# A decoder layer on one core: the first feed-forward product made as features by tokens, with its layer norm applied behind the second product

## The chip, the core and the metric

The kernel runs on one core of a Trainium2 chip. A core has TensorE (PE: matrix products into PSUM; PEld is its loading of weights), VectorE (DVE), ScalarE (ACT), GpSimd (POOL, which reaches SBUF but not PSUM) and SyncE (SP, which here issues DMAs). Each engine works through its own instructions in their order and waits on semaphores for the others. The metric is the device time of one execution in microseconds; the median of the runs shown counts.

## What is computed

x is 128 sequences of 128 tokens by 256 features; ctx has the same shape. The layer is self-attention, cross-attention and a feed-forward part, each on a layer norm of x and each added to x; both attentions have 16 heads of 16 features. The part that matters here, cut from the reference:

```python
def layernorm(x, w, b, eps=LN_EPS):
    mu = jnp.mean(x, axis=-1, keepdims=True)
    var = jnp.mean((x - mu) ** 2, axis=-1, keepdims=True)
    return (x - mu) * jax.lax.rsqrt(var + eps) * w + b
h = jnp.einsum('btd,hd->bth', x, absmean(W_fc))      # 256 -> 1024
h = jax.nn.gelu(h, approximate=False)
h = layernorm(h, ln_w, ln_b)                         # over the 1024
return jnp.einsum('bth,dh->btd', h, absmean(W_proj)) # 1024 -> 256
```

absmean makes a matrix of −1, 0 and 1 from the weights. The layer norm stands between the two products, over the 1024 hidden features of each token.

## The kernel before

The 128 sequences are taken in 32 groups of G = 4 rows, a row being one sequence of 128 tokens. The kernel is written as streams (Python generators), each of which issues a few instructions and yields: A is the attention of all groups, one row at a time, first the maxima of the scores (`maxima`, L680), then transposed scores (L752), exponentials (`weights`, L778) and outputs (L797); n prepares a group for self-attention, k the keys and values of the context, c the queries of the cross-attention, and f (`finish`, L581) projects the cross-attention's result, adds it to x and does the feed-forward part; w and t prepare constants and weights; x, y and z (`finish_rows`, L608) do the feed-forward part of the last group in pieces of 2, 1 and 1 rows.

The order of all work is written out by hand as strings of these letters: `START + ORDER * (n_groups - 4) + END` (L860). So ORDER is repeated 28 times, and within each engine the instructions stand in the order of the letters. Nothing is reordered later. In one repetition 36 steps of A, 36 steps of f (before) and the steps of n, k and c alternate, so that the attention of one group runs beside the feed-forward part of an earlier one.

PSUM has eight banks. Two tiles of two banks hold scores, one bank holds the attention's outputs, and three banks (`bank`, L194) serve every other product in turn; a product can start only when the bank that it gets has been read.

The feed-forward part of a group, before, has two pairs of rows:

- `transposed` (L290) computes the layer norm of x (statistics on VectorE, rstd and `apply` on GpSimd, L281, L282 and L286) and transposes the result on TensorE (pt, L304). `split` (L429) makes two parts of it, a rounded one (fp32r) and its remainder, so that products in fp32r keep their precision.
- `hidden` (L434) makes the first product tokens by features: the 128 tokens of a row are the stationary operand, 512 columns of `w_fc` the moving one, four matmuls per bank (two parts by two chunks of 128 input features, L443). ScalarE applies gelu from PSUM into g (L450). VectorE takes the statistics of g over the 1024 features (L275, L276), GpSimd makes rstd, and g is normalised in place, row 0 by VectorE and row 1 by GpSimd (L286).
- `second` (L469) transposes g in blocks of 128 by 128 on TensorE into PSUM (pg, L477; 16 per pair). From there ScalarE writes the rounded part times ln_w (L486) and VectorE the remainder (L488, one input from PSUM, one from SBUF). Sixteen matmuls per row of these parts with `w_proj` (py, L501) make the result, and VectorE adds it to x (L510). ln_b times `w_proj` is the constant row `b_proj` (L537 to L547), added by GpSimd (`add_row`, L421).

Gelu and Exp need different tables on ScalarE. The kernel asks for Gelu's at L438 and Exp's at L452; where a function follows that isn't in the table that is loaded, the build puts in a further load.

All transfers but two at the start are issued by SP, in the order of the letters: per group the next x, the context, the rearrangement of the attention's outputs (sums, o_raw), the factors by way of DRAM (by_head, factors) and the output (L602).

Of the kernel before, what the change touches and what calls it, by code (L numbers as in the profile page):

```python
# [27 lines left out]
P = 128  # L28
D = 256
# [24 lines left out]
    "nnnnnnwnwnnnwnnnAnAAnnAwnAAnAnAnAAAAAnnAAknnwAnnnnwnccnkAnnAAnnAnAkAcccckcAAcAnAAkccAccccntAAkAAnkAn"  # L54
    "AnAAnAkckAnnAnAcAnAnAnntAnAAAckccAccckkAAknAkAnknAnckcnAcAActAAftkAAAncAcAAntAAAffffAffnAnfnAnnAAnAn"
    "kAffnAAkfcfAffkfAAfknncffAAffffAkkfAnfcAcnfAfAffAAccfAc"
)
ORDER = (
    "ncfAfffAAkkAccAAcfcAnnfAAAccAffAAnnkAAnnAnfAnkAAAfffAfffnAAkcnnAnnAnAfkfkcAffffffAAfffAfffAfccccfffA"
    "fkfkAAAncfAn"  # L60
)
END = (
    "cfAfAffAfAcAcffcAfAAckAAxcAkcfffAAfffAAkfAAAAAkffkAcfAcAfffffAffAffccfffAcckcfckfAffAfAkkAfcAcfAAffc"
    "cAcfcAfAfkAAffAkAkfkAAAAfAfAffffAAxxAffAxAfffAxfffyfAfffffyfxAyffffAfxyxxxzxyfxfffzffyxzzffxxxxyyzxx"
    "yyzzzyzzz"
# [4 lines left out]
def tile_decoder_layer(ctx: ExitStack, tc: tile.TileContext, a: dict, out: bass.AP):  # L70
# [55 lines left out]
    with nc.allow_non_contiguous_dma(reason="a few hundred bias elements, once"):  # L126
# [18 lines left out]
        for src, shape in ((a["w_fc_t"], [P, CC, FF]), (a["w_proj_t"], [P, FC, D])):  # L145
            raw = p_one.tile(shape, F32, name="raw_w", tag="g", bufs=2)
            nc.sync.dma_start(raw, src.rearrange("(c p) o -> p c o", p=P))
            raw_weights.append(raw)
# [66 lines left out]
    def output_bias(w):  # L215

        pb = bank("pb")
        bv_cols = p_one.tile([P, CC, P], F32, name="bv_cols", tag="g_0")
# [5 lines left out]
    def masks():  # L224
        ident_32 = p_one.tile([P, 32], F32, name="ident_32", tag="g_0")
# [208 lines left out]
    def hidden(xn_parts, j0, n_rows=2, at=0):  # L434

        terms = [(i, c) for c in range(CC) for i in range(2)]
        g = p_one.tile([P, 2, FF], F32, name="g", tag="g", bufs=2)
        nc.scalar.preload_act_table(AF.Gelu)  # L438
        for j in range(n_rows):
            for n in range(FF // 512):  # L440
                ph = bank("ph")
                for i, c in terms:
                    nc.tensor.matmul(  # L443
                        ph,
                        xn_parts[i][:, c, (j0 + j - at) * P : (j0 + j - at + 1) * P],
                        w_fc[:, c, n * 512 : (n + 1) * 512],
# [3 lines left out]
                nc.scalar.activation(g[:, j, n * 512 : (n + 1) * 512], ph, AF.Gelu)  # L450
                if j + n == n_rows:
                    nc.scalar.preload_act_table(AF.Exp)  # L452
                yield
        agg = p_stat.tile([P, 2, 2], F32, name="agg", tag="agg", bufs=6)
        if n_rows == 2:
# [13 lines left out]
    def second(x, g, j0, n_rows=2):  # L469
# [29 lines left out]
        for j in range(n_rows):  # L499
# [8 lines left out]
            if j < n_rows - 1:  # L508
                yield
# [396 lines left out]
```

## Time and profile before

| what | us |
|---|---|
| median of 3 runs (lowest, highest) | 2737.69 (2736.14, 2737.96) |
| span of the profiled execution, first to last instruction | 2733.8 |
| TensorE busy | 2676.2 (98%) |
| VectorE busy | 2118.7 (78%) |
| ScalarE busy | 1579.2 (58%) |
| GpSimd busy | 1337.1 (49%) |
| length of one repetition of ORDER | 82.8 |

The profiled execution has no time of its own beside its span; the median is 3.9 us above that span. A row of the groups of instructions reads: line, engine, operation, what it writes and reads, the count, then busy time, mean length of one in ns, and the idle time just before them with what ended it. In a timeline a row is the start in us, the length, engine, line and operation; xN joins N instructions that follow each other. Means of matmuls overlap, since one starts before the former has ended; the distance of their starts is what one costs.

### The profile page before, as it was taken

The numbers are of one execution on the slowest core, as the hardware profiler recorded it, in microseconds if no ns is written. First come the engines' busy times: TensorE is split into PE (matmuls) and PEld (weight loads), VectorE is DVE, ScalarE is ACT, GpSimd is POOL, SyncE is SP. The second block draws the span as 40 slices with busy tenths as digits, with TensorE's granted clock in tenths as the row PEclk, the third lists the DMA queues.
The fourth block names the chain that finished last, engine by engine and source line by source line (L and its number), as shares of the span: only waits on it lengthen the run. The fifth ranks groups of instructions, "written<-read, shape, count | busy, mean of one in ns | idle before, by whom it ended". The sixth has DMA issues, their size and how long they took to land.

```text
span 2733.8 us, 77048 instructions
## 1 busy us (share of the span) xinstructions
PE 2676.2 (98%) x32845; PEld 1917.3 (70%) x32845; DVE 2118.7 (78%) x3916; ACT 1579.2 (58%) x2508; POOL 1337.1 (49%) x1425
## 2 busy tenths in 40 slices
PE   7999999999999999999999999999999999999998
PEld 4567777677777767776777776777777777777666
DVE  5677787777787777887777887777877778877777
ACT  3455666655665655665556666556656556665446
POOL 3344554544554554554445545445545445545443
PEclk9999999999999999999999999999999999999999
DMA  4121111221111221122211112211112211212210
GB/s 118 33 50 42 41 41 50 57 57 34 46 44 50 57 58 28 46 49 51 58 42 41 42 50 57 58 42 42 42 49 58 58 31 44 49 49 50 50 26 16
DMA packets 110093, 130.28 MB, mean 48 GB/s; under 512 B 32312, under 2 KB 69048, under 8 KB 109752
## 3 DMA queue, kind: packets, MB, share of 16 engines
q1 hardware_dynamic: 109464, 125.11, 19.0%
q8 instruction: 259, 4.24, 0.6%
q14 instruction: 82, 0.67, 0.1%
q10 hardware_dynamic: 288, 0.26, 0.0%
HBM read 71.38 MB, written 18.84 MB: 33 GB/s over the span
## 4 chain that ended last, share of the span: by engine, by line
PE 89%; DVE 7%; issue 2%; POOL 1%; ACT 1%; DMA 0%; ACTq 0%; DVEq 0%; SPq 0%; POOLq 0%
PE st L761 10%; PE av L806 9%; PE pq L324 9%; PE s L700 9%; PE ph L443 9%; PE py L501 8%; PE pk L324 8%; PE po L336 8%; PE pv L336 8%; PE pt L304 3%; PE pg L477 2%; PE s L689 2%; PE st L785 2%; DVE mx L711 1%; DVE g L488 1%
## 5 line engine op out<-in xcount | busy, mean ns | idle before, releaser
L711 DVE TENSOR_REDUCE mx<-s 128x8 f32<-128x1024 f32 x512 | 601.3, 1216 | 83.0 <-PE s L700 82.5
L794 ACT ACTIVATE w_t<-st 128x1024 f32<-128x1024 f32 x512 | 496.7, 1022 | 202.5 <-PE st L785 122.3
L281 POOL TENSOR_SCALAR rstd<-agg 128x4 f32<-128x4 f32 (+2 forms) x163 | 39.0, 239 | 965.5 <-DVE agg L276 965.5
L286 POOL TENSOR_SCALAR xn<-x,agg,rstd 128x256 f32<-128x256 f32 x378 | 458.4, 1226 | 9.9
L771 DVE COPY_PREDICATED_SCALAR st<-masked_t,masked_score 128x1024 f32 x256 | 316.1, 1280 | 68.1 <-PE st L761 68.1
L414 POOL TENSOR_TENSOR o_raw<-o_raw,factors 128x256 f32<-128x256 f32 x252 | 181.0, 745 | 382.9 <-DMA factors<-by_head 277.0
L809 ACT COPY raw<-av 128x512 f32<-128x512 f32 x256 | 151.0, 590 | 315.3 <-PE av L806 310.4
L486 ACT ACTIVATE g<-pg,ln_w 128x256 fp32r<-128x256 f32 (+1 forms) x520 | 205.8, 473 | 175.8 <-PE pg L477 163.6
L700 PE MATMUL s<-kt,qt 32*128 32x256 f32 x4096 | 298.8, 402 | 3.2 <-ACT w_t L794 2.2
L501 PE MATMUL py<-w_proj,g 128*128 128x256 f32 x2048 | 279.6, 289 | 1.3 <-DVE g L488 0.8
L806 PE MATMUL av<-w_t,v 128*32 128x128 f32 x8192 | 276.9, 276 | 0.5 <-DVE q_max L733 0.5
L806 PEld LDWEIGHTS av<-w_t,v 128*32 128x32 f32 x8192 | 209.0, 109 | 96.7 <-issue 80.0
L443 PE MATMUL ph<-w_fc,xn 128*128 128x512 f32 x1024 | 259.8, 404 | 4.2 <-ACT g L450 1.6
L501 PEld LDWEIGHTS py<-w_proj,g 128*128 128x128 f32 x2048 | 254.1, 189 | 13.2 <-issue 1.3
L286 POOL TENSOR_SCALAR g<-g,agg,rstd 128x1024 f32<-128x1024 f32 x63 | 241.1, 3828 | 6.6
L488 DVE SCALAR_TENSOR_TENSOR g<-pg,ln_w,g 128x256 fp32r<-128x256 f32 (+1 forms) x520 | 212.6, 469 | 30.3 <-ACT g L486 29.9
L700 PEld LDWEIGHTS s<-kt,qt 32*128 32x128 f32 x4096 | 187.8, 185 | 63.7 <-issue 40.2
L443 PEld LDWEIGHTS ph<-w_fc,xn 128*128 128x128 f32 x1024 | 184.8, 188 | 58.7 <-DVE xn L432 10.0
L761 PEld LDWEIGHTS st<-q_max,kt 32*128 32x128 f32 x4096 | 129.2, 186 | 61.1 <-DVE negm_self L722 42.5
L275 DVE BATCH_NORM_STATS2 stats<-g 128x6 f32<-128x512 f32 x256 | 160.9, 670 | 0.8 <-ACT g L450 0.8
L450 ACT ACTIVATE g<-ph 128x512 f32<-128x512 f32 x256 | 146.5, 599 | 25.3 <-PE ph L443 24.2
L761 PEld LDWEIGHTS st<-qt,kt 32*128 32x128 f32 x4096 | 128.1, 186 | 46.3 <-DVE mx L711 26.4
(130 smaller groups left out, 4612.8 us busy)
## 6 DMA issues: line engine op xcount, KB each, us to landing
o_raw<-raw SPq DMA_DIRECT2D x504, 64.0 KB
factors<-by_head SPq DMA_DIRECT2D x126, 256.0 KB
ctx_t<-in_ctx_t_dram SPq DMA_DIRECT2D x32, 512.0 KB
x<-in_x_dram SPq DMA_DIRECT2D x31, 512.0 KB
out_dram<-x SPq DMA_DIRECT2D x31, 512.0 KB
sums<-raw SPq DMA_DIRECT2D x126, 16.0 KB
by_head<-r SPq DMA_DIRECT2D x63, 32.0 KB
raw_w<-in_w_fc_t_dram SPq DMA_DIRECT2D x1, 1024.0 KB
```

The source lines that it names most:

```text
L286: engine.tensor_scalar(dst[:, j], src[:, j], agg[:, j, 0:1], rstd[:, j : j + 1], ALU.subtract, ALU.mult)
L324: nc.tensor.matmul(out, w[:, c, o * P : (o + 1) * P], src_t[:, c], start=(c == 0), stop=(c == CC - 1))
L336: nc.tensor.matmul(rows[:, j], src_t[:, c, (j0 + j) * P : (j0 + j + 1) * P], w[:, c], start=(c == 0), stop=(c == CC - 1),)
L443: nc.tensor.matmul(ph, xn_parts[i][:, c, (j0 + j - at) * P : (j0 + j - at + 1) * P], w_fc[:, c, n * 512 : (n + 1) * 512], start=((i, c) == ...
L488: nc.vector.scalar_tensor_tensor(parts[1][:, f0 + f, tok], pieces[:, f], scales[f], parts[0][:, f0 + f, tok].bitcast(F32), ALU.mult, ALU.s ...
L501: nc.tensor.matmul(rows[:, j], parts[i][:, f, j * P : (j + 1) * P], w_proj[:, f], start=((i, f) == terms[0]), stop=((i, f) == terms[-1]),)
L700: nc.tensor.matmul(s[r // 2][:, r % 2, 2 * o : 2 * o + 2], qt[strip, o, tok], kt[strip, o, :, tok], start=(stage == "self"), stop=True, sk ...
L711: nc.vector.tensor_reduce(mx[:, 2 * half : 2 * half + 2], s[half], AX.X, ALU.max, negate=True)
L761: nc.tensor.matmul(s[r // 2][:, r % 2, n], kt[strip, n // 2, n % 2, tok], added[strip, n // 2, n % 2] if stage == "self" else qt[strip, n ...
L771: nc.vector.copy_predicated(s[half].rearrange("p r n q -> p (r n) q"), masked_t[:, None, :].to_broadcast([P, 8, P]), masked_score[:, :, No ...
L794: nc.scalar.activation(w_t[:, 2 * half : 2 * half + 2], s[half], AF.Exp)
L806: nc.tensor.matmul(av[32 * r : 32 * r + 32, n], v[:, j, head : head + 32], w_t[:, r, n], start=True, stop=True)
```

## The change

The first product is turned round. The weights `w_fc` are now the stationary operand, in blocks of 128 hidden features, and the 256 tokens of a pair of rows the moving one, so that the result in PSUM is features by tokens and g comes out as the second product needs it: there is no transpose of g. Since the layer norm is over the features, which now lie along the partitions, it moves behind the second product: with shift = −mean, the result is (h·ln_w·w_proj + shift·w_sum)·rstd + b_proj, where `w_sum` is the row ln_w times `w_proj`, made once.

```diff
-        g = p_one.tile([P, 2, FF], F32, name="g", tag="g", bufs=2)
         nc.scalar.preload_act_table(AF.Gelu)
-        for j in range(n_rows):
-            for n in range(FF // 512):
-                ph = bank("ph")
+        for f0 in range(0, FC, n_f):
+            ph = bank("ph")
+            for f in range(n_f):
                 for i, c in terms:
                     nc.tensor.matmul(
-                        ph,
-                        xn_parts[i][:, c, (j0 + j - at) * P : (j0 + j - at + 1) * P],
-                        w_fc[:, c, n * 512 : (n + 1) * 512],
+                        ph[:, f * width : (f + 1) * width],
+                        w_fc[:, c, (f0 + f) * P : (f0 + f + 1) * P],
+                        xn_parts[i][:, c, tok],
...
-                nc.scalar.activation(g[:, j, n * 512 : (n + 1) * 512], ph, AF.Gelu)
...
-            statistics(g, (0,), FF, agg)
...
-            apply(nc.gpsimd, g, g, agg, rstd, 1)
...
-        apply(nc.vector, g, g, agg, rstd, 0)
...
+            g = p_one.tile([P, 512], F32, name="g", tag="g", bufs=4)
+            nc.scalar.activation(g, ph, AF.Gelu)
+            for f in range(f0, f0 + n_f):
+                piece = g[:, (f - f0) * width : (f - f0 + 1) * width]
+                scale = ln_w[:, f : f + 1]
+                nc.scalar.activation(parts[0][:, f, 0:width], piece, AF.Copy, scale=scale)
                 nc.vector.scalar_tensor_tensor(
-                    parts[1][:, f0 + f, tok],
-                    pieces[:, f],
-                    scales[f],
-                    parts[0][:, f0 + f, tok].bitcast(F32),
+                    parts[1][:, f, 0:width],
+                    piece,
+                    scale,
+                    parts[0][:, f, 0:width].bitcast(F32),
                     ALU.mult,
                     ALU.subtract,
                 )
+            if f0 == 0:
+                nc.scalar.activation(totals[:, 1], g, AF.Square)
+                before = g
+            else:
+                squares = p_one.tile([P, 512], F32, name="sq", tag="sq", bufs=2)
+                nc.scalar.activation(squares, g, AF.Square)
+                nc.gpsimd.tensor_tensor(totals[:, 0], before, g, ALU.add)
+                nc.gpsimd.tensor_tensor(totals[:, 1], totals[:, 1], squares, ALU.add)
+                before = totals[:, 0]
+            if f0 + n_f == FC:
+                nc.scalar.preload_act_table(AF.Exp)
             yield
+        while n_f > 1:
+            n_f //= 2
+            half = n_f * width
+            for i in range(2):
+                nc.gpsimd.tensor_tensor(
+                    totals[:, i, 0:half], totals[:, i, 0:half], totals[:, i, half : 2 * half], ALU.add
+                )
+        return parts, totals
+
+    def moments(totals, n_rows=2):
+
+        sums = bank("sums")[:, 0 : 2 * n_rows * P].rearrange("p (i j t) -> p i j t", i=2, j=n_rows)
+        for i in range(2):
+            for j in range(n_rows):
+                nc.tensor.transpose(sums[:, i, j], totals[:, i, j * P : (j + 1) * P], ident)
+        total = p_stat.tile([P, 2, n_rows], F32, name="total", tag="total", bufs=1)
+        nc.vector.tensor_reduce(total, sums, AX.X, ALU.add)
+        shift = p_stat.tile([P, n_rows], F32, name="shift", tag="shift", bufs=2)
+        nc.vector.tensor_scalar(shift, total[:, 0], -1.0 / FF, None, ALU.mult)
+        square = p_stat.tile([P, n_rows], F32, name="square", tag="square", bufs=1)
+        nc.vector.tensor_tensor(square, shift, shift, ALU.mult)
+        nc.vector.scalar_tensor_tensor(square, total[:, 1], 1.0 / FF, square, ALU.mult, ALU.subtract)
+        rstd = p_stat.tile([P, n_rows], F32, name="rstd", tag="rstd", bufs=6)
+        nc.gpsimd.tensor_scalar(rstd, square, 0.0, LN_EPS, ALU.max, ALU.add)
+        nc.gpsimd.tensor_tensor(rstd, rstd, minus_half.to_broadcast([P, n_rows]), ALU.pow)
+        return shift, rstd
...
-                    nc.tensor.transpose(
-                        pieces[:, f, j * P : (j + 1) * P],
-                        g[:, j, (f0 + f) * P : (f0 + f + 1) * P],
-                        ident,
-                    )
...
-        nc.vector.tensor_tensor(x[:, j0 : j0 + n_rows], x[:, j0 : j0 + n_rows], rows, ALU.add)
+            yield
+        shift, rstd = moments(totals, n_rows)
+        yield
+        for j in range(n_rows):
+            nc.vector.scalar_tensor_tensor(
+                rows[:, j], w_sum, shift[:, j : j + 1], rows[:, j], ALU.mult, ALU.add
+            )
+            nc.vector.scalar_tensor_tensor(
+                x[:, j0 + j], rows[:, j], rstd[:, j : j + 1], x[:, j0 + j], ALU.mult, ALU.add
+            )
```

So after each gelu ScalarE writes the rounded part of two blocks and the square of g, VectorE writes the remainders, and GpSimd adds up g and its squares over the eight blocks. The matmuls of the second product (py) follow, then `moments` transposes the totals, VectorE sums them up, GpSimd makes rstd, and four operations of VectorE per pair bring the result into x. The bank of py is held until then.

`finish` now runs `hidden` and `second` of the first pair, then of the second; before, it ran `hidden` of both pairs and then `second` of both. The f stream has 26 steps per group instead of 36, and all three strings of letters are new:

```diff
 ORDER = (
-    "ncfAfffAAkkAccAAcfcAnnfAAAccAffAAnnkAAnnAnfAnkAAAfffAfffnAAkcnnAnnAnAfkfkcAffffffAAfffAfffAfccccfffA"
-    "fkfkAAAncfAn"
+    "nkAfAcAAfnfAAkcfAcnckAAcfcAAAcknAkAnnAfffAAnnAAnfAfAfnfcnAnnAAnfkAnAfknfAfcfAAffccAfAfnfAffkAAAffcccA"
+    "fk"
 )
...
-        gs = []
         for j0 in range(0, G, 2):
-            gs.append((yield from hidden(xn_parts, j0)))
-        for j0, g in zip(range(0, G, 2), gs):
-            yield from second(x, g, j0)
+            parts, totals = yield from hidden(xn_parts, j0)
+            yield from second(x, parts, totals, j0)
```

The preparation of the ternary weights works in pieces of 512 columns instead of whole matrices, with other buffers, and makes `w_sum` beside `b_proj` (16 more matmuls, once). In the last group's pieces of one row a bank of ph holds four blocks of 128 columns.

## The prediction

> **What bounds the kernel now.** I read the page's first two parts, then the groups by shape, then a stretch of the repeated order and the timelines of ScalarE, VectorE and GpSimd in it. TensorE is the limit: busy 98% of the span, at full clock in all 40 slices.
>
> ```profile
> span 2733.8 us, 77048 instructions
> PE 2676.2 (98%) x32845; PEld 1917.3 (70%) x32845; DVE 2118.7 (78%) x3916; ACT 1579.2 (58%) x2508; POOL 1337.1 (49%) x1425
> PEclk9999999999999999999999999999999999999999
> ```
>
> One repetition of ORDER (28 of them) is a window of 82.85 us, in which TensorE idles 0.36 us; the others have room on average (columns: length, then busy time of PE, PEld, DVE, ACT, POOL):
>
> ```profile
> 1356.60:1439.45 82.85, 82.49 (x1029) 59.28 (x1025) 65.18 (x120) 49.22 (x79) 41.58 (x44) 1.00 0.18 45
> ```
>
> So time taken from TensorE is gained in full, if nothing in the new order makes it wait. These groups are touched (count | busy us, mean ns | idle before); a mean overlaps its neighbour, so I price matmuls by the spacing of starts:
>
> ```profile
> L477 PE MATMUL pg<-ident,g 128*128 128x128 f32 x1024 | 142.1, 276 | 3.6 <-DVE g L286 2.0 <-DVE g L488 1.2 <-DVE xn L432 0.4
> L443 PE MATMUL ph<-w_fc,xn 128*128 128x512 f32 x1024 | 259.8, 404 | 4.2 <-ACT g L450 1.6 <-DVE v L372 1.2 <-DVE g L488 1.1
> L501 PE MATMUL py<-w_proj,g 128*128 128x256 f32 x2048 | 279.6, 289 | 1.3 <-DVE g L488 0.8 <-ACT g L450 0.5
> L286 POOL TENSOR_SCALAR g<-g,agg,rstd 128x1024 f32<-128x1024 f32 x63 | 241.1, 3828 | 6.6
> L414 POOL TENSOR_TENSOR o_raw<-o_raw,factors 128x256 f32<-128x256 f32 x252 | 181.0, 745 | 382.9 <-DMA factors<-by_head 277.0 <-issue 105.0
> L438 ACT ACT_TABLE_LOAD x65 | 83.4, 1283 | 1.1
> ```
>
> Two places show something that the averages hide. While weights are prepared, VectorE runs an operation with two inputs in SBUF beside a GpSimd add or product with two inputs in SBUF:
>
> ```profile
> 120.60 3.61 POOL L414 TENSOR_TENSOR o_raw<-o_raw,factors 128x256 f32<-128x256 f32 x2 [2.24 <-DMA factors<-by_head]
> 120.93 2.70 DVE L535 SCALAR_TENSOR_TENSOR w_fc<-raw_w,half,below 128x2048 fp32r<-128x2048 f32 x1
> 161.48 3.28 POOL L414 TENSOR_TENSOR o_raw<-o_raw,factors 128x256 f32<-128x256 f32 x3 [9.02 <-DMA factors<-by_head]
> 161.91 1.56 DVE L540 TENSOR_TENSOR b<-ln_b,b 128x1024 fp32r<-128x1024 f32 x1
> ```
>
> Alone, the second L535 (w_proj) took 2.35 us and a GpSimd product 0.73. Here L535 took 0.35 more, what was left of the first product; the second product then waited until L535 had ended at 123.63: 3.61 us for what otherwise takes 1.46. At 161.9 it happens again. So these two kinds of instruction exclude each other, and take turns. The kernel before hardly ever mixes them: its L488 reads one input from PSUM.
>
> **The change, part by part** (per repetition, thus per group of four rows).
>
> TensorE: 32 transposes pg go, at 0.118 us (4 from 1457.31 to 1457.75, 8 from 1453.42 to 1454.39): −3.8. The 32 ph matmuls of 512 columns at 0.2425 (16 from 1439.40 to 1443.28), 7.8 us, become 64 of 256 columns. Nearest row: py, also 256 columns, 0.121 to 0.136 per matmul; I take 0.125, 8.0 us (ends 7.7 to 8.7). Eight transposes of totals add 0.9. Net −2.6 (−2.9 to −1.9): 80.25 us if TensorE never waits.
>
> VectorE: statistics of g (8 × 0.64 + 4 × 0.2 us) and its apply (2 × 1.0) go, −7.9; the wide add into x (2 × 0.69) becomes eight 256-wide operations at 0.45 and, twice, one reduction (0.65, as the 512-wide L510) and three tiny operations at 0.16: +4.3. Net −3.6 of 65. The 16 operations that make parts[1] keep their 0.42 us, but now read both inputs from SBUF.
>
> ScalarE: eight squares at about 0.55 (spacing of the 512-wide gelus) add 4.4. The built program has 193 table loads instead of 131, two more per repetition, because an Exp of the attention now falls between the third and fourth gelu of the second pair: +2.6. The copies read SBUF instead of PSUM; no row shows that, so 0.365 (spacing of L486) to 0.47 (its length) each, and I take the former. 49.2 becomes about 56.
>
> GpSimd: the applies of g go, −7.6; 12 additions of 512 columns come at 1.22 to 1.46 (256 columns take 0.73, of which up to 0.24 may be fixed, as in L281), I take 1.25; plus four of 256: +18. 41.6 becomes about 52.
>
> On average all fit into 80. But these pieces lie in the first 38 us after a group's first ph, where TensorE's order has this without waits (us after that ph): four ph steps until 6.1, py j=0 8.1 to 10.2, py j=1 10.5 to 12.5, totals 13.5; second pair ph 15.1, 19.3 to 21.3 and 23.5, py 27.5 to 29.5, pn 31.6, py 31.8 to 33.9, pt 37.4. I followed what each waits for:
>
> 1. First pair, ScalarE: load done at 1.5; each step holds it 1.86 (gelu 0.6, two copies 0.365, square 0.5), raw 0.59 between: third gelu ends at 6.35, and po waits for its bank: 0.25 lost.
> 2. First pair, sharing: from the second gelu's end (3.95) GpSimd has 9.0 us of additions, and VectorE six parts[1] operations among them. If a pair of these goes between two additions, the last ends near 11.5 where py j=0 wants it by 10.1, and the additions end at 15.6: about 1.85 lost. In strict turns the last ends at 14.8: about 4.7.
> 3. Second pair: x is now updated by four operations (1.9 us) after a reduction, and behind them on VectorE stand two parts[1] operations and the masking (2 × 1.25) that releases the attention's st: 0.7 lost.
> 4. Then on ScalarE, from the third ph's end (20.8): gelu step 1.86, gelu step 1.96, load 1.28, two Exp 1.94, load 1.28, gelu 0.6 is 8.9, ready 29.7. py, whose bank that gelu empties, would come at 28.4: 1.3 lost. Behind it queue the Exps for the next av.
> 5. The maxima L711 (2.35) stand behind the last parts[1]: 0.7, with sharing 1.35.
> 6. Statistics of the next x come behind those; GpSimd's rstd (1.3) and four applies (4.85) make xn 0.85 late for pt.
>
> Without sharing 3.8 us; with pairs 6.3; with strict turns, followed through the second pair too, 10.2. The rows say that turns are taken, but not whether VectorE keeps the port for two in a row; its L488 operations start 0.39 apart (four in 1.65 us) though 0.47 long, so I put the sum near the lower of the two: 7.0. Repetition: 80.25 + 7.0 = 87.25, that is +4.4; 28 × 4.4 = +123. The rest of a repetition has slack: there every wait in the order is met before its time by this addition. On SP's queue the output DMA waits later with x (VectorE ready 44 us after the first ph); by_head and factors of the next projection queue behind it, and are first needed 10 us later: nothing.
>
> Outside ORDER: three groups in START and END gain 2.6 each if not held up, −8; w_sum costs 16 matmuls (2.4) and 2.7 us on VectorE once, +4; the last pieces lose a statistics and eight transposes for additions on GpSimd, ±5. Sum −4, with ±15.
>
> Sum: the profiled span 2733.8, and 3.9 around it to the median of the three runs, 2737.7. 2737.7 + 123 − 4 = 2857.
>
> One rule speaks against the change still more. The row first: 65 table loads took 1283 ns each with 1.1 us idle before all of them, and the gelu follows within 0.01 us. The Trainium skill, "ScalarE: Activation LUTs", section "What ACT_TABLE_LOAD costs", adds a drain of about 1380 ns to each switch. By it, the two further loads of item 4 would cost 2.8 us more in each repetition, 28 × 2.8 = 77, and the estimate would be 2934; the trace shows no drain, and the sum leaves it out.
>
> **The rivals.**
> - Strict turns: 80.25 + 10.2 is +7.6 per repetition, 2947. For it: the second product waited out all of L535. Against: no row has two VectorE operations queued.
> - No sharing of note, only ScalarE's chain (items 1, 3 to 6): 84.05, +1.2 × 28 − 4, 2767. For it: L771 with two constants in SBUF keeps 1.21 to 1.29 beside GpSimd work.
> - Faster: the waits are absorbed, because ScalarE's steps from SBUF overlap more than PSUM's rows show and py finds its pieces. It decides below 2.6 us lost per repetition, at item 4 first; with half of that lost 2697, with none 2661. For it: VectorE and GpSimd are lighter or idle on average; TensorE certainly gets less work.
> - The transposes don't go: no; 1024 become 256, that is in the program.
>
> **How the numbers follow.** Forecast 0.42 (own range 2800 to 2915, for 5 to 9 us lost per repetition), strict turns 0.16, chain alone 0.18, faster 0.20, within 0.2% (about what a measurement of this kernel can tell from no change) 0.04. Slower 0.76. The range from 2690 to 2955 leaves out about half of the faster case and the end of strict turns.
>
> **What would show it.** Right: pg gone and TensorE's busy time near 2600, but a repetition of 87 us; waits of py for parts[1] and gelu and of st for maxima near 5 us a repetition; the parts[1] operations well above 0.47 and GpSimd's additions well above 1.25 in the mean; 193 loads. Wrong: the additions at 1.25 with parts[1] at 0.42 (no sharing), or TensorE still busy 98% (faster).

## The result: 3038 us, 11% slower

The changed kernel takes 3037.93 us (median of 4 runs, 3034.3 to 3044.72), the kernel before 2736.91 on the same chip (4 runs, 2735.74 to 2737.96). The ratio is 1.1104, 95% interval 1.1088 to 1.1120. The forecast was 2857, between 2690 and 2955: the sign was right, and the size of the loss, +120, was less than half of the real +301.

The page of the changed kernel, busy times and the clock:

```profile
span 3038.1 us, 78178 instructions
PE 2765.2 (91%) x33149; PEld 1980.1 (65%) x33149; DVE 2286.5 (75%) x3933; ACT 1821.3 (60%) x2826; POOL 1704.5 (56%) x1878
PEclk9999999999999999999999999999999999999988
```

TensorE now idles 273 us of its span, and although it has less to do it is busy 89 us longer. The row of the clock hides a part of why, since 9 stands for anything from 0.9. The records of the clock behind it have 42 stretches at 0.50, 239 us of the span, where the kernel before had 10 us. At half clock the matmuls of py start 0.21 us apart instead of 0.12, and all that time counts as busy.

One repetition of ORDER, from the Gelu load of one group (L445) to that of the next, is the same length of order as the 82.85 us shown of before (length, then busy time of PE, PEld, DVE, ACT, POOL, then the clock, the share of the DMA engines and GB/s):

```profile
1397.22:1489.94 92.72, 85.38 (x1033) 61.02 (x1033) 70.29 (x121) 56.89 (x89) 53.22 (x58) 0.96 0.17 43
```

Measured so, the mean of 27 repetitions is 82.83 us before and 91.97 after. That is +9.14 each, +256 for all 28, of the 304 by which the span is longer. The other 48 lie in START and END. In a repetition after, TensorE is busy 84.87 us and idle 7.10, where before it was 82.49 and 0.35.

The groups that the change made, by shape:

```profile
L463 DVE SCALAR_TENSOR_TENSOR g<-g,ln_w,g 128x256 fp32r<-128x256 f32 x504 | 464.3, 970 | 70.7 <-ACT g L462 70.7
L516 PE MATMUL py<-w_proj,g 128*128 128x256 f32 x2048 | 373.3, 331 | 86.1 <-DVE g L463 81.9 <-DVE x L530 2.3 <-DVE x L417 0.8
L478 POOL TENSOR_TENSOR totals<-totals,sq 128x512 f32<-128x512 f32 x191 | 255.5, 1338 | 17.8 <-ACT sq L476 17.6 <-DMA by_head<-r 0.2
L826 ACT ACT_TABLE_LOAD x31 | 39.8, 1283 | 2.3 <-DVE st L803 1.7
L458 ACT ACT_TABLE_LOAD x31 | 39.8, 1283 | 0.6
```

The operation that made parts[1] before:

```profile
L488 DVE SCALAR_TENSOR_TENSOR g<-pg,ln_w,g 128x256 fp32r<-128x256 f32 x504 | 208.3, 474 | 27.6 <-ACT g L486 27.2
```

L463, which makes parts[1] now, lasts 970 ns in the mean; its predecessor L488 lasted 474. L478, an addition, lasts 1338 ns in the mean, little more than the 1.28 us that it takes alone. So most of the waiting is VectorE's. TensorE's own waits, longest first (us in total, times, longest):

```profile
PE py L516 <- DVE g L463: 81.9, 142, 1.9
PE pv L335 <- DVE x L417: 67.9, 27, 2.6
PE pt L303 <- POOL xn L285: 33.0, 65, 0.9
PE st L793 <- DVE mx L743: 16.1, 33, 1.3
PE st L817 <- DVE st L803: 13.5, 15, 2.7
PE po L335 <- POOL o_raw L413: 13.0, 12, 2.4
```

Now the first pair of one repetition, VectorE first and then GpSimd in the same stretch of the timeline:

```profile
1404.08 2.46 DVE L803 COPY_PREDICATED_SCALAR st<-masked_t,masked_score 128x1024 f32 x2
1406.46 4.15 DVE L463 SCALAR_TENSOR_TENSOR g<-g,ln_w,g 128x256 fp32r<-128x256 f32 x4
```

```profile
1405.25 1.30 POOL L478 TENSOR_TENSOR totals<-totals,sq 128x512 f32<-128x512 f32 x1
1406.50 1.55 POOL L477 TENSOR_TENSOR totals<-totals,g 128x512 f32<-128x512 f32 x1
1408.01 1.45 POOL L478 TENSOR_TENSOR totals<-totals,sq 128x512 f32<-128x512 f32 x1
1409.42 1.77 POOL L487 TENSOR_TENSOR totals<-totals 128x256 f32<-128x256 f32 x2
```

Four L463, 1.65 us of work (as four L488 took before), take 4.15 us: one gets through before L477 of 1406.50, and then one between each two additions. These are strict turns. The additions give up little: the longest here takes 1.55 us, 0.27 more than alone. TensorE meets the turns at py of this pair:

```profile
1406.98 0.50 PE L516 MATMUL py<-w_proj,g 128*128 128x256 f32 x2 [0.17 <-DVE g L463]
1408.39 0.51 PE L516 MATMUL py<-w_proj,g 128*128 128x256 f32 x2 [0.91 <-DVE g L463]
1409.80 0.67 PE L516 MATMUL py<-w_proj,g 128*128 128x256 f32 x2 [0.90 <-DVE g L463]
1410.66 0.58 PE L516 MATMUL py<-w_proj,g 128*128 128x256 f32 x1 [0.20 <-DVE g L463]
1411.18 0.61 PE L817 MATMUL st<-negm_t,add_max 32*128 32x128 bf16 x16
1411.72 3.78 PE L516 MATMUL py<-w_proj,g 128*128 128x256 f32 x16
```

The first row of py (16 matmuls) takes from 1405.48 to 1411.2, where 2.0 would do. The second row has every piece it needs, waits for nothing, and still takes 3.6 us to the next product's start instead of 2.0. The windows of that stretch show why (the clock is the last but two of the columns):

```profile
1406.00:1408.00 2.00, 1.30 (x9) 0.90 (x8) 2.00 (x3) 1.98 (x3) 2.00 (x2) 1.00 0.00 0
1408.00:1410.00 2.00, 0.71 (x3) 0.50 (x4) 2.00 (x3) 0.46 (x2) 2.00 (x3) 0.99 0.00 0
1410.00:1412.00 2.00, 1.80 (x20) 1.09 (x20) 1.67 (x4) 0.44 (x2) 2.00 (x4) 0.50 0.00 0
1412.00:1414.00 2.00, 2.00 (x10) 2.00 (x11) 0.15 (x1) 1.98 (x3) 1.95 (x3) 0.50 0.00 0
```

TensorE was busy 1.30 and 0.71 of 2 us, and from 1409.96 on its clock is 0.50, for 6.8 us, while it is fully busy again. The clock falls like this behind the first pair in 27 places of the repetitions.

### The profile page after: what moved, and what is told of

It reads as the page before. It is cut to its first block, busy times and chain, and to the rows that moved or that the text cites. A ratio compares the mean times of both kernels' runs of the same rounds, so it can differ in the third digit from the quotient of the medians.

```text
span 3038.1 us, 78178 instructions
## 1 busy us (share of the span) xinstructions
PE 2765.2 (91%) x33149; PEld 1980.1 (65%) x33149; DVE 2286.5 (75%) x3933; ACT 1821.3 (60%) x2826; POOL 1704.5 (56%) x1878
## 5 line engine op out<-in xcount | busy, mean ns | idle before, releaser
L463 DVE SCALAR_TENSOR_TENSOR g<-g,ln_w,g 128x256 fp32r<-128x256 f32 (+1 forms) x520 | 473.2, 959 | 75.3 <-ACT g L462 75.3
L285 POOL TENSOR_SCALAR xn<-x,agg,rstd 128x256 f32<-128x256 f32 x378 | 458.2, 1224 | 10.2
L516 PE MATMUL py<-w_proj,g 128*128 128x256 f32 x2048 | 373.3, 331 | 86.1 <-DVE g L463 81.9
L516 PEld LDWEIGHTS py<-w_proj,g 128*128 128x128 f32 x2048 | 313.2, 225 | 141.2 <-DVE g L463 115.8
L803 DVE COPY_PREDICATED_SCALAR st<-masked_t,masked_score 128x1024 f32 x256 | 316.0, 1279 | 86.7 <-PE st L793 86.7
L450 PE MATMUL ph<-xn,w_fc 128*128 128x256 f32 (+1 forms) x2080 | 289.5, 290 | 1.4 <-DVE o_raw L665 0.7
L450 PEld LDWEIGHTS ph<-xn,w_fc 128*128 128x128 f32 x2080 | 259.4, 193 | 31.2 <-issue 11.5
L478 POOL TENSOR_TENSOR totals<-totals,sq 128x512 f32<-128x512 f32 x191 | 255.5, 1338 | 17.8 <-ACT sq L476 17.6
L477 POOL TENSOR_TENSOR totals<-g 128x512 f32<-128x512 f32 x65 | 83.7, 1288 | 296.0 <-ACT g L458 296.0
L462 ACT ACTIVATE g<-g,ln_w 128x256 fp32r<-128x256 f32 (+1 forms) x520 | 234.0, 498 | 8.3
L477 POOL TENSOR_TENSOR totals<-totals,g 128x512 f32<-128x512 f32 x126 | 175.6, 1394 | 97.8 <-ACT g L458 97.8
L335 PE MATMUL pv<-xattn_wv,ctx_t 128*128 128x256 f32 x512 | 138.4, 393 | 68.2 <-DVE x L417 67.9
```

The lines of the kernel that those rows point to most:

```text
L285: engine.tensor_scalar(dst[:, j], src[:, j], agg[:, j, 0:1], rstd[:, j : j + 1], ALU.subtract, ALU.mult)
L450: nc.tensor.matmul(ph[:, f * width : (f + 1) * width], w_fc[:, c, (f0 + f) * P : (f0 + f + 1) * P], xn_parts[i][:, c, tok], start=((i, c) ...
L462: nc.scalar.activation(parts[0][:, f, 0:width], piece, AF.Copy, scale=scale)
L463: nc.vector.scalar_tensor_tensor(parts[1][:, f, 0:width], piece, scale, parts[0][:, f, 0:width].bitcast(F32), ALU.mult, ALU.subtract,)
L477: nc.gpsimd.tensor_tensor(totals[:, 0], before, g, ALU.add)
L478: nc.gpsimd.tensor_tensor(totals[:, 1], totals[:, 1], squares, ALU.add)
```

## The experiments

The theory (T in the expectations): VectorE's L463 and GpSimd's additions exclude each other in turns; TensorE waits at py; the low load halves its clock. The rival (A): ScalarE's longer chain of gelu, copies, squares and table loads. The runs, each beside one run of the kernel before (2735.6 to 2740.6); a repetition is the mean of 27, half clock is the sum in us over 28 repetitions. L463 has another line number in some of these kernels. Every kernel below the second was run once; the four runs of the changed kernel lie 10 us apart, so a difference of 20 us from it says little more than its sign.

| kernel | us | repetition | half clock | mean L463, ns |
|---|---|---|---|---|
| before | 2736.9 | 82.8 | 1 | (L488) 474 |
| changed | 3037.9 | 92.0 | 171 | 970 |
| no_adds | 2807.0 | 84.8 | 3 | 484 |
| pool_one_input | 2801.3 | 84.6 | 3 | 502 |
| filler | 3024.3 | 91.1 | 79 | 974 |
| no_switch | 3018.4 | 91.1 | 160 | 945 |
| rest_from_psum | 3014.4 | 92.1 | 157 | 479 |
| adds_on_vector | 2984.2 | 90.0 | 113 | 483 |
| late_py | 3150.6 | 95.8 | 294 | 1017 |
| adds_vector_swap_rounded_first | 2987.8 | 90.2 | 143 | 481 |
| adds_256 | 2924.7 | 88.5 | 79 | 706 |
| adds_128 | 3003.6 | 91.2 | 123 | 564 |
| adds_256_x_first | 2932.0 | 88.7 | 82 | 663 |
| adds_256_x_first_rounded_first | 2938.3 | 89.1 | 85 | 662 |
| adds_256_plain_update | 2863.5 | 86.7 | 0 | 686 |
| no_norm | 2731.2 | 82.8 | 7 | 484 |
| no_norm_squares | 2793.6 | 84.7 | 41 | 485 |

### The additions: left out, or with one input

```diff
-                nc.gpsimd.tensor_tensor(totals[:, 0], before, g, ALU.add)
-                nc.gpsimd.tensor_tensor(totals[:, 1], totals[:, 1], squares, ALU.add)
-                before = totals[:, 0]
```

> The additions of g and of its squares on GpSimd (L477, L478, L487) are left out; the squares are still made, and the last g and the first squares are transposed instead of the totals. Theory T (turns): VectorE's L463 with two inputs in SBUF and GpSimd's additions exclude each other in strict turns, TensorE waits at py, and the low load then halves its clock. Without additions L463 is back near 0.45 us, no clock is lost within the repetitions, and a repetition is near 84 us: 2767, between 2720 and 2800. Rival A (ScalarE): the longer chain of gelu, copies, squares and table loads is what py waits for; it is all still there: above 2950.

```diff
+                nc.gpsimd.tensor_scalar(totals[:, 0, 0:256], g[:, 0:256], 0.0, 1.0, ALU.max, ALU.add)
+                nc.gpsimd.tensor_scalar(totals[:, 1, 0:256], squares[:, 0:256], 0.0, 1.0, ALU.max, ALU.add)
```

> Each GpSimd addition of 512 columns (1.34 us) becomes an operation with one input in SBUF over 256 columns (such as L285, 1.22 us), each of 256 columns one of 128; so GpSimd is as busy as before, but with one input. The totals are wrong. Theory T in its narrow form (only two inputs on both sides exclude each other): L463 near 0.45 us and 2770 to 2810. Theory T in its wide form (any GpSimd operation that reads SBUF excludes a VectorE operation with two inputs there, as the Trainium skill, SBUF: State Buffer, has it): L463 stays near 0.95 us and the time within 2% of 3038. Rival A: within 2% of 3038, but with L463 near 0.45 us.

Measured 2807, 7 us above the range, and 2801, in it. Without the additions 231 of the 301 us are gone, and with GpSimd nearly as busy as in the changed kernel (1601 us, 1704 there) 237 are. In the second kernel, by shape:

```profile
L463 DVE SCALAR_TENSOR_TENSOR g<-g,ln_w,g 128x256 fp32r<-128x256 f32 x504 | 229.7, 502 | 131.4 <-ACT g L462 131.4
L478 POOL TENSOR_SCALAR totals<-sq 128x256 f32<-128x256 f32 x191 | 228.0, 1194 | 48.7 <-ACT sq L476 48.3 <-DMA by_head<-r 0.4
```

VectorE no longer waits, so it is not GpSimd's load that counts but what its operation reads: one input instead of two. (The new operation also has half the columns and another function; that VectorE with one SBUF input is not held up either is shown by rest_from_psum below.) ScalarE's chain is the same in both runs, so the rival is not the main cause.

The Trainium skill, "SBUF — State Buffer", section "SBUF: two separate sides", gives the lock: a VectorE operation with two SBUF inputs and a GpSimd operation that reads SBUF hold a shared port for a whole instruction, and whoever comes second blocks. The turns of the changed kernel agree. Taken literally it also covers a GpSimd operation with one input, and there the measurement decides. L463 takes 502 ns against 484 in no_adds, and 513 in the mean where it starts during a GpSimd operation. It is GpSimd that is held up: its operations of 256 columns (L477 and L478) take 1.07 us where they meet no L463, and 1.45 in the mean, up to 1.90, where they meet three.

### The clock: filler for TensorE

```diff
+                if j0 == 0 and n_rows == 2 and j == 0 and i == 1 and f > 1:
+                    for _ in range(6):
+                        nc.tensor.matmul(
+                            rows[:, 1], parts[0][:, f, P : 2 * P], w_proj[:, f], start=False, stop=False
+                        )
```

> In the first pair, six matmuls of 256 columns whose result is overwritten stand ahead of each remainder's matmul of py's first row from the third hidden block on, so TensorE has 36 more matmuls (4.5 us) where it waited 3.7. No other engine's work changes. If the halved clock comes from the low load of TensorE, the half-clock stretch of 6.8 us behind the first pair's py goes in most repetitions, which gives 3.4 us back, less up to 1 us for filler that does not fit into the waits: 2945, between 2920 and 2990, with the mean clock above 0.98. If the clock falls for another reason (heat, or the kind of work), the filler only adds: 3038 to 3070 at 0.96.

Measured 3024: the mechanism came true, the size did not. Of the 27 falls of the clock behind the first pair none is left, with nothing changed but TensorE's load, and py's second row takes 2.2 us in the mean instead of 3.6. But behind the second pair, where TensorE waits for pv's bank, they rose from 6 to 18, so the half clock went from 171 to 79 us only, not to about nothing. That is 46 us of work at most. The filler that did not fit took some 19 of it: py's first row lasts 6.3 us in the mean instead of 5.6. The falls behind the second pair follow a wait of up to 2.6 us in one piece:

```profile
PE pv L335 <- DVE x L417: 68.7, 27, 2.6
```

The clock changes on a grid of 3.413 us: all its changes in the changed kernel lie on multiples of it to within 1 ns, and in the repetitions every half-clock stretch there is one or two steps long (up to three in late_py). From 200 to 2500 us of the changed kernel, worked out from the records of TensorE and its clock: a step at full clock in which TensorE was busy 0.52 or less was followed by half clock in 22 of 22 cases, 0.52 to 0.64 in 8 of 34, more in 0 of 572. In the same stretch of all 17 kernels it is 253 of 298, 52 of 191 and 4 of 10559 (three of the four in no_norm_squares, at 0.67 and 0.68). So the share decides nearly always, but no one value of it does. Once the clock is halved a busy step does not always restore it: of the 46 steps at half clock in the changed kernel, all busier than 0.64, 16 were followed by another.

The longest single idle time in most of the steps that led to half clock is 0.9 us. The Trainium skill, "TensorE: Matmul & The Clock Gate", section "HAM oscillation — how this bites in real kernels", gives as the rule that no idle gap may exceed about 3.4 us. Here gaps of 0.9 us were enough, since it is the share of the step that counted: single gaps of 1.2 to 1.6 us in steps busy 0.53 to 0.64 were not followed by half clock in the changed kernel.

### ScalarE: two table loads less

```diff
-            nc.scalar.activation(g, ph, AF.Gelu)
+            last = j0 == 2 and n_rows == 2 and f0 + n_f == FC
+            nc.scalar.activation(g, ph, AF.Copy if last else AF.Gelu)
...
-            if f0 + n_f == FC:
+            if f0 + n_f == FC and not last:
```

> The last gelu of each second pair is a plain copy, which needs no table: two of six table loads per repetition go (2.6 us of ScalarE), nothing else changes but the values of a quarter of that pair's hidden features. Theory T: what ends TensorE's waits is VectorE, so little comes back: 3000 to 3038. Rival A: the loads lie on the path that py of the second pair waits for, with 1.3 us per repetition by the prediction's item 4 and more where it was too small: below 2990, and py's wait in the second pair gone.

Measured 3018, as the theory has it: 20 us, 0.7 per repetition (0.9 by the two traces).

### VectorE's side: the remainder from PSUM

```diff
-                    piece,
+                    ph[:, (f - f0) * width : (f - f0 + 1) * width],
```

> L463 takes its first input from ph in PSUM instead of g in SBUF, so VectorE reads one input from SBUF, as L488 did in the kernel before; GpSimd's additions stay as they are. The remainders are wrong, and ph's bank is held until L463 has read it. Narrow form of theory T (two inputs in SBUF on both sides): L463 near 0.47 us, additions near 1.28 us, hardly any half clock in the repetitions: 2790 to 2860, the upper part for the banks held longer. If an addition excludes VectorE whatever it reads, L463 stays near 0.95 us and the time within 2% of 3038.

Measured 3014, and it hit neither: L463 is at 479 ns and L478 at 1278, so the turns are gone as the narrow form says, but the time is not. ph's bank is now held until L463 has read it, and the product that gets this bank next waits:

```profile
PE po L335 <- DVE g L463: 74.5, 29, 2.6
```

Another 56 us of po's waits stand under L477, but there too po starts 0.1 us after an L463 ends (1125.89 and 1125.79 in one repetition).

Taking the turns away is not enough if the cure holds one of three banks for longer.

### The additions on VectorE

```diff
+    def add_owed(totals, owed):
+        for before, g, squares in owed:
+            nc.vector.tensor_tensor(totals[:, 0], before, g, ALU.add)
+            nc.vector.tensor_tensor(totals[:, 1], totals[:, 1], squares, ALU.add)
+        owed.clear()
...
+            add_owed(totals, owed)
...
-                nc.gpsimd.tensor_tensor(totals[:, 0], before, g, ALU.add)
-                nc.gpsimd.tensor_tensor(totals[:, 1], totals[:, 1], squares, ALU.add)
+                owed.append((before, g, squares))
...
-                nc.gpsimd.tensor_tensor(
+                nc.vector.tensor_tensor(
```

> The additions go from GpSimd to VectorE, each pair of them behind the remainders of the next step; the computation is whole. On one engine there is nothing to exclude; VectorE has 12 more operations of 512 columns (0.68 us, as L417) and 4 of 256 (0.45) per repetition, 10 us on top of some 62 of 84. Theory T: L463 near 0.48 us, no half clock in most repetitions, and a repetition between the 84.2 without additions and 2.5 us more for remainders, masking and maxima that now stand behind additions: 2880, between 2820 and 2950. If VectorE has no room, more than 2950.

Measured 2984, beyond the range: the second case, that VectorE has no room. No L463 waits for a turn (483 ns), and of py's 82 us of waits for it 3 are left. But VectorE has 262 us of additions of 512 columns and 49 of 256 in place of the 245 us that it lost in turns (504 times 486 ns), in the same stretch, and TensorE waits for what stands behind them:

```profile
PE pt L303 <- POOL xn L285: 61.4, 97, 0.9
PE pv L335 <- DVE x L417: 47.6, 27, 1.8
PE st L800 <- DVE mx L750: 38.1, 57, 1.5
PE sums L504 <- DVE totals L494: 27.3, 32, 3.3
```

With the last gelu ahead of the exponentials (no table switch) and py's rounded parts first:

```diff
-    "nkAfAcAAfnfAAkcfAcnckAAcfcAAAcknAkAnnAfffAAnnAAnfAfAfnfcnAnnAAnfkAnAfknAfcfAAffccAfAfnfAffkAAAffcccA"
-    "fk"
+    "nkAfAcAAfnfAAkcfAcnckAAcfcAAAcknAkAnnAfffAAnnAAnfAfAfnfcnAnnAAnfkAnAfknAfcfAAffccAfAfnfAffkAAAffcccf"
+    "Ak"
...
-        for j in range(n_rows):
-            for i, f in terms:
+        for i in range(2):
+            for j in range(n_rows):
+                for f in range(FC):
```

> As adds_on_vector, with two more edits. In the order, the last gelu step of the second pair stands ahead of the exponentials that stood before it, so both table loads go (0.9 us per repetition by no_switch); and py takes the rounded parts of both rows first, then the remainders of both, so the remainders are wanted 2 us later. Theory T: 1.5 to 3 us per repetition below adds_on_vector, 2810, between 2750 and 2880. If VectorE's additions are what TensorE waits for at the maxima and the masking, less than 0.5 us per repetition below adds_on_vector.

Measured 2988, nothing gained. The exponentials, one gelu step later, now make the next scores wait (97 us, s behind w_t).

### The order: py later

```diff
-    "nkAfAcAAfnfAAkcfAcnckAAcfcAAAcknAkAnnAfffAAnnAAnfAfAfnfcnAnnAAnfkAnAfknAfcfAAffccAfAfnfAffkAAAffcccA"
+    "nkAfAcAAfnfAAkcfAcnckAAcfcAAAcknAkAnnAfffAAnnAAnfAfAfnfcnAnnAAnfkAnAfknAfcfAAffccAAnAfffffkAAAffcccA"
```

> Only the order changes: one step of values (four matmuls) and one of self-attention scores (16) of TensorE, which stood behind py of the first pair, stand ahead of it, 2.3 us at full clock. Theory T: the wait for the turns, some 4.6 us per repetition, shrinks by 2.3, and most windows of TensorE stay above the load at which the clock halves, 3.0 more: 2890, between 2870 and 2960. If the clock falls all the same, 2975.

Measured 3151, the worst run, against 2890 expected, and 2975 had the clock fallen all the same. The scores that were moved ahead of py write the tiles that ScalarE's exponentials have just got to read:

```profile
PE s L732 <- ACT w_t L826: 139.9, 32, 5.3
```

A new wait of 5 us in one piece, at the start of the step that was to fill a wait. That TensorE had other work to put there was an assumption; the order leaves no such slack.

### Shorter turns

```diff
-                nc.gpsimd.tensor_tensor(totals[:, 0], before, g, ALU.add)
-                nc.gpsimd.tensor_tensor(totals[:, 1], totals[:, 1], squares, ALU.add)
+                for at in range(0, 512, 256):
+                    part = slice(at, at + 256)
+                    nc.gpsimd.tensor_tensor(totals[:, 0, part], before[:, part], g[:, part], ALU.add)
+                    nc.gpsimd.tensor_tensor(totals[:, 1, part], totals[:, 1, part], squares[:, part], ALU.add)
```

> Each addition of 512 columns on GpSimd (1.28 us alone) becomes two of 256 (0.73 each, by L487 and L413); the computation is the same, and GpSimd's time rises by 2 us per repetition. Theory T, strict turns: an L463 waits for the rest of one addition, now at most 0.73 us: its mean falls from 0.97 to 0.70 to 0.80. Of the 7.7 us per repetition that turns and clock cost together, 3 to 5 come back: 2920, between 2890 and 2960. If VectorE gets its turn only when GpSimd's queue is empty, or if GpSimd's load as such counts, 3030 or more.

The same with pieces of 128 columns:

> As adds_256, with four additions of 128 columns each (0.49 us, of which 0.24 fixed, by the rows of 256 and 512 columns): GpSimd's time rises by 9 us per repetition. Strict turns: L463 at 0.60 to 0.70, a repetition at 86 to 87 if the additions still end before the totals are transposed: 2880, between 2850 and 2930. If they end too late, waits of sums for GpSimd show and the time lies above adds_256.

Measured 2925 and 3004. L463 is at 706 ns with halves and 564 with quarters, as strict turns have it: it waits for the rest of one addition. With halves 113 us of the 301 come back, with the same computation. With quarters (488 ns each) GpSimd ends too late, the second of the two cases written down beforehand:

```profile
PE sums L499 <- POOL totals L489: 94.9, 55, 3.8
```

### The second wait: x's addition behind the remainders

With halves the longest wait is that of pv for L417, the addition of po into x, which empties the bank that pv gets. In the changed kernel it stood behind four L463, which took 3.6 us:

```profile
1427.42 3.60 DVE L463 SCALAR_TENSOR_TENSOR g<-g,ln_w,g 128x256 fp32r<-128x256 f32 x4
1430.95 0.67 DVE L417 TENSOR_TENSOR x<-x,po 128x512 f32<-128x512 f32 x1
```

Both orders below put two of the four behind it, on top of adds_256; the second also takes py's rounded parts first.

```diff
-    "nkAfAcAAfnfAAkcfAcnckAAcfcAAAcknAkAnnAfffAAnnAAnfAfAfnfcnAnnAAnfkAnAfknAfcfAAffccAfAfnfAffkAAAffcccA"
+    "nkAfAcAAfnfAAkcfAcnckAAcfcAAAcknAkAnnAfffAAnnAAnfAfAfnfcnAnnAAnfkAnAfknAfcfAAffccAfAfnfAffkAAAfcccfA"
```

> As adds_256, and in the order the third step of the second pair's first product stands behind the three steps of the next group's projection instead of ahead of them; so on VectorE the addition into x (L417), which empties po's bank, stands ahead of two of the four L463 that held it back. If that queue is what pv of the context waits for (62 us in adds_256, 2.2 per repetition), 1 to 1.5 us per repetition of that go, less up to 0.7 that the later gelu costs py of the second pair: 2900, between 2880 and 2925. If po's bank comes free late for another reason, the wait stays and the time is 2925 or more.

> As adds_256_x_first, and py takes the rounded parts of both rows first, then the remainders of both: its first 16 matmuls (2 us) no longer wait for L463. Turns are taken as before, but 21 us of py's waits for L463 in adds_256 go, and some half-clock stretches with them: 1 us per repetition below adds_256_x_first, 2870, between 2850 and 2900. If the waits only move to the next step (the rounded parts then wait for ScalarE's copies, or the projection for its bank), within 10 us of adds_256_x_first.

Measured 2932 and 2938. The wait has not gone, it only has another name, ph for L417 (71 us): VectorE works without a break from the totals' reduction to L417, 12 us after the former's start, and one step earlier in the queue does not help. So its load in that stretch was tested. The totals are left unread and x is updated by one addition per pair:

```diff
-        shift, rstd = moments(totals, n_rows)
+        moments(totals, n_rows)
...
-            nc.vector.scalar_tensor_tensor(
-                rows[:, j], w_sum, shift[:, j : j + 1], rows[:, j], ALU.mult, ALU.add
-            )
-            nc.vector.scalar_tensor_tensor(
-                x[:, j0 + j], rows[:, j], rstd[:, j : j + 1], x[:, j0 + j], ALU.mult, ALU.add
-            )
+        nc.vector.tensor_tensor(x[:, j0 : j0 + n_rows], x[:, j0 : j0 + n_rows], rows, ALU.add)
```

> As adds_256, but the totals are transposed and then left unread (no reduction, shift or rstd), and x takes py by one addition per pair: the layer norm is left out of the result. VectorE loses 2.4 us per pair (a reduction of 0.68, three of 0.16, four of 0.48, less one of 0.68), which stood ahead of the second pair's masking, remainders and the addition into x. If VectorE's queue in that stretch is the second cause beside the turns, pv's wait for that addition (62 us) and most of the 75 us of half clock behind it go: 3 us per repetition, 2840, between 2810 and 2870. If the addition into x is late for another reason, 2900 or more.

Measured 2863: 61 us less than adds_256, and in the range, though with 1.8 per repetition instead of 3. The wait falls from 62 to 20 us and no half clock is left in the repetitions:

```profile
PE pv L335 <- DVE x L417: 20.1, 27, 0.8
```

So the moved layer norm's own work behind py, 2.4 us per pair on VectorE with GpSimd's rstd between, is the second cause; the edit takes out both, and does not tell them apart. It counts only on top of the additions: without them the same work costs 0.1 us per repetition (the sum of steps below).

### The turned product alone

Squares, additions, transposes of totals, moments and the four-operation update are left out, the table loads and the order stay; then the squares are put back.

```diff
-        shift, rstd = moments(totals, n_rows)
...
+        nc.vector.tensor_tensor(x[:, j0 : j0 + n_rows], x[:, j0 : j0 + n_rows], rows, ALU.add)
```

> Only the turned product, without any layer norm: squares, additions, transposes of totals, moments and the four-operation update are left out; x takes py by one addition. What this run is below the changed kernel is the price of the moved layer norm. If TensorE's saved work is real and only the statistics cost, a repetition falls to TensorE's work, 80 to 81.5 us, with the two table loads still there: 2690, between 2665 and 2730, below the kernel before. If the order or the table loads hold it, above 2740.

> As no_norm, with the squares back on ScalarE (8 per repetition, 4.4 us), which nothing reads. What it is above no_norm is the squares' share by way of ScalarE: 0.5 us per repetition by the prediction's item 4, thus 2705, between 2690 and 2735; nothing if ScalarE has room there.

Measured 2731, between the two cases written down, and 2794, above the range. TensorE's saving is real, in no_norm:

```profile
PE 2608.7 (96%) x32893; PEld 1879.4 (69%) x32893; DVE 1893.9 (69%) x3482; ACT 1690.2 (62%) x2570; POOL 1027.6 (38%) x1232
```

It is busy 67 us less than before. But the span is only 4.5 us shorter, since it idles 121 us instead of 58: 43 us at pt for xn (4 before), 21 at py for gelu, 15 at po for o_raw. So even without any layer norm this order gives the kernel nothing to speak of. The squares cost 62 us more by way of ScalarE, far more than the 15 expected: the exponentials come late for the next scores (23 us), po waits (8), and 34 us more at half clock follow.

The steps add up per repetition: 82.8 without statistics, +1.9 for squares, +0.1 for moments, update and transposes (no_adds), +7.2 for the additions on GpSimd, 92.0.

## Why the prediction was wrong

The sign came from the right mechanism, and the rows that carried it, L414 beside L535 while weights are prepared, were read rightly: two inputs in SBUF on both engines exclude each other. The step that failed is the last of the sum, 80.25 + 7.0 = 87.25. It takes TensorE's own work as the same whether or not TensorE waits. The waits came to 7.1 us per repetition, as forecast. But TensorE was busy 84.9, not 80.25. Up to 3.1 of these 4.6 us are the half clock (6.2 us of it per repetition); 1.3 are there in no_adds and pool_one_input too, which have next to no half clock and are busy 81.6 and 81.5. What makes these 1.3 is open.

That the waits met the 7.0 is luck, for the parts did not. Point by point:

- TensorE's matmuls were priced rightly: 16 of ph take 2.0 us, 0.125 each. Its busy time near 2600 did not come: it is 2765, of which the half clock explains 119 at most, and 2661 in no_adds. It is 2609 only in no_norm, which also lacks the eight transposes.
- Without sharing the sum gave 84.05 per repetition; no_adds and pool_one_input measured 84.8 and 84.6. The sum held better than its parts: TensorE idles 3.2 and 3.1 us there where the items gave 3.8, and its longer busy time makes up for it. Item 1 (po, 0.25) is there, 28 times 0.3 us; the profile does not name what po waits for, but the wait comes with the squares and is not in no_norm. Item 4 was 1.3 and measures 0.8 (21 us of py's waits for gelu in no_adds; no_switch gave 0.7 to 0.9). Item 5 was 0.7 and measures nothing in no_adds (5.0 us of st's waits for the maxima in all, 4.9 before); with sharing it was 1.35 and measures 0.6. Item 6 was 0.85 and measures 1.2, of which 0.1 was there before; but it is there in no_norm too, so its cause was not the queue behind the moments.
- Item 2 chose the wrong case. The text let the row of L488 starts decide for pairs between turns. A row of an operation that never met the conflict cannot say how it is resolved. The rows that did meet it showed GpSimd, with more products queued, giving way after a single one; they showed nothing of two operations queued on VectorE. The rival "strict turns" (2947, chance 0.16) had the right case, but at the wrong price: 10.2 us of waits per repetition where 7.1 came, and 91 us short all the same. Of those 7.1, py waits 2.5 for L463.
- Item 3 priced the right queue with the wrong victim. It followed VectorE's queue to the masking and st (13.5 us, 0.5 per repetition), and not to the addition into x behind the same L463, whose bank pv waits for: 67.9 us, 2.4 per repetition.
- What TensorE's clock does when TensorE waits has no item at all. The prediction read the clock at full in all 40 slices of a kernel that hardly idles, and carried 1.00 over to one that it forecast to wait 7 us per repetition. 171 us at half clock in the repetitions cost up to 85 us, and 54 us more behind them up to 27. In the repetition shown, 3.7 us lost in py's first row were followed by 6.8 us at half clock, up to 3.4 lost again.
- "Outside ORDER" was −4 with ±15, and is +45 of the 301. no_adds, 71 us longer in span than before, has 16 there and 55 in its 28 repetitions, so about 30 are the additions again, in stretches that the prediction took to be uncovered but harmless.
- VectorE's own list adds up to +4.5 and not +4.3; nothing hangs on it.

From 2857 to 3038: up to 85 by the clock in the repetitions, 49 outside ORDER, and some 47 more in the repetitions, nearly all of it the rest of TensorE's longer busy time. The clock's part is an upper bound, since TensorE also waited in some of those stretches, and the last part is what remains.

No version that computes the whole beat the kernel before. The best is adds_256, 2925, 3.7% below the changed kernel and 6.9% above the one before; no_norm, which computes less, shows that little could be gained with this order. Whether an order made anew, with the turns and the clock in its costs, could keep TensorE's saving stays open.

## What to carry to other kernels

Before work goes to GpSimd, look at what VectorE does at the same time: if both have two inputs in SBUF, each VectorE operation waits for what is left of GpSimd's, and they take turns. One SBUF input on either side ended VectorE's waits here, and GpSimd operations of half the length shortened them; look at what the cure holds up in its place. Price a wait of TensorE with the clock: when it was busy less than about half of a 3.4 us step, the next step or two mostly ran at half clock. Filler matmuls prevented that, though here they took back some 19 of the 46 us at most that they gave. When a dense order is disturbed, follow every bank to the operation that empties it, for that operation's place in its engine's queue is what the next product waits for.

## What the runs showed of the hardware that was not expected

- The length of the GpSimd operation sets the loss of VectorE almost alone: L463 takes 970, 706 and 564 ns beside additions of 512, 256 and 128 columns (1.28, 0.73 and 0.46 us alone), and 484 without them. The additions of 512 columns last 1.29 to 1.39 us in the mean, 9% more than alone at most.
- GpSimd operations of 1.07 us with one SBUF input leave VectorE at 502 ns, and are held up themselves, to 1.45 us in the mean where they meet three L463.
- TensorE's clock falls by the share of a 3.41 us step, not by the longest gap: 0.9 us gaps at a share of 0.42 were followed by 6.8 us at half clock in one repetition after the other.
- The gelu after a table load starts 0.02 us after the load's end (load at 1397.22 for 1.28, gelu at 1398.52), and two loads fewer gave 0.7 to 0.9 us per repetition, where they last 2.6: nothing was seen of a drain beside them.
